# An attention and feed-forward block on one core: where the last splits of x are traced, and the last feature blocks of gate and up as a seven-product pair

## The chip, the cores and the metric

The kernel runs on one core of a Trainium2 chip. The metric is device time in microseconds, the median over runs. All arithmetic is float32; matmuls take their operands as float32 with rounded mantissa ("fp32r"), and a product that must be exact to float32 is made of three of them.

## The reference

One token block of 2048 rows (T) and 1024 columns (C) goes through an attention layer and a feed-forward layer, each with a layer norm ahead of it, a layer norm behind it and a residual:

```
x = x + layernorm(attention(layernorm(x)))   # one head, width 256
x = x + layernorm(ffn(layernorm(x)))
ffn(x) = (silu(x @ W_gate.T) * (x @ W_up.T)) @ W_down.T   # 2752 features
```

The feed-forward width of 2752 is 21 blocks of 128 features and a last piece of 64.

## The kernel before

**Three-fold products.** Every operand is split into a high part (a cast to fp32r, on ScalarE) and a low part (the source minus the high part, on VectorE). A block of a product is then three matmuls: high by high, high by low, low by high (`mmc`, L600 to L607, whose matmul is L605). The weight splits stand in `split` (L109 cast, L110 subtraction), those of x in `split_later` (L407 cast, L408 subtraction), whose two instructions are kept in their traced order against other work (`pin`).

**Stages.** First come q, k and v, then attention over 16 row tiles (`scores`, `softmax`, `turn`, `attend`, `turn_o`, `proj`), then, for each half s of the rows, gate and up (`gate_up`, then `gate_up_rest`) and the down product (`run_down`). The residual and layer norm of the last eight attention tiles run as background jobs inside the first half's gate and up. An instruction scheduler sets the final order on every engine from the traced order and its own estimates; each engine then works through its queue in order, and waits where an operand isn't ready.

**Seven products instead of eight.** A pair of feature blocks (p and p + 10) by two halves of rows and two halves of the inner dimension is a 2 x 2 by 2 x 2 block product. `gate_up` makes it with seven block products (Strassen's scheme in a form with few sums): the weight sums S1 to S4 are made on chip in `Pair.prep` (L529 to L532), the sums of x are called T1 to T4, the plain blocks A11 to A22 and B11 to B22. A `prod` is 4 inner blocks by 3 matmuls of 512 columns, 12 matmuls, into one PSUM bank. Gate and up of one pair are 14 `prod` calls over the four banks `ag`, `au`, `cg`, `cu`. Ten pairs cover 20 blocks. What is left over, block 20 of gate, block 20 of up, and the 64 last features of gate and of up side by side in one block (`wlast`), is done in `gate_up_rest` as three `Single` blocks with four `prod` calls each.

**Buffers of weights.** Split weights lie in six slots (four in `a2`, shown as `a`, and two in `wvo`, which held Wo during attention), raw weights in the four buffers `f4[4]`, `f2p[0]`, `f2p[1]`, `wr[0]` (shown as f, f2p, wr). A queue of loads and preparations (`Feeder`) is pumped whenever a slot comes free, at each `done()`.

**Buffers of x.** The split x of the current half lies in `xb` (B11, B21), `kx` (T1, T3), `qa` and `qb` (T2) and `a1` (T4, B22; shown as `a`, as `a2` is). `kx`, `qa`, `qb` and `a1` hold attention's keys, queries and values until it ends. For the first half, sums of x made during attention are stored to memory (`xs_d`), and ten pieces (`First` objects, in the list `order`) are loaded and split late: `order[0:4]` before the last `attend`, `order[4:6]` ahead of `turn_o(15)` and `proj(15)`, `order[6:10]` behind `proj(15)` and ahead of the first pair. They pass through four buffers, f4[2], f4[3], wr[1] and xe (`spare`). `order[4]` fills `qb`, `order[5]` the last of T1 and T3, `order[6:10]` T4 and B22.

**Names in the profile.** L276 and L277 are matmuls of `attend`, L279 and L280 gather its result, L285 is `turn_o`, L146 to L148 with wvo are `proj`, and L295 is its scaling and bias. L637 and L639 are the ScalarE copies that free banks `ag` and `au` after the first two products of a pair; L651 to L664 are the later copies, L618 is every sum on VectorE, L621 every silu, L347 the transposes of a background job.

Of the kernel before, what the change touches and what calls it, by code (L numbers as in the profile page):

```python
# [11 lines left out]
ALU = mybir.AluOpType  # L12
# [3 lines left out]
P = 128  # L16
# [10 lines left out]
FR = F - FB * P  # L27
NKB = T // P
EPS = 1e-5
NPAIR = 10  # L30
# [4 lines left out]
def block_kernel(ctx, tc, x, wqk, wv, bqk, bv, wo, bo, wgu, wlast, wd, out):  # L35
# [12 lines left out]
    nc = tc.nc  # L48
# [13 lines left out]
    bo_s = tl(cpool, [P, C], F32, "bo_s")  # L62
# [25 lines left out]
    hl_d = [[tl(dram, [FR, 512], F32, f"hl_d{s}_{k}") for k in range(2)] for s in range(2)]  # L88
# [5 lines left out]
    f4 = [tl(cpool, [P, C], F32, f"f4_{i}") for i in range(5)]  # L94
# [325 lines left out]
    class First:  # L420


        def __init__(self, dst, halves):
            self.dst, self.halves = dst, halves
# [69 lines left out]
    class Pair:  # L494


        def __init__(self, p, m):
            self.p, self.m = p, m
            self.s = {}
            one, two_, three, four = Slot(), Slot(), Slot(), Slot()  # L500
            self.slot = [one, two_, three, four]

            self.at = {"A11": (one, 0), "A12": (one, 4), "S2": (two_, 0), "S1": (two_, 4), "S3": (three, 0), "S4": (three, 4), "A22": (four, 0)}
# [3 lines left out]

        def load(self):
            self.r = [raws.get(), raws.get()]
            for r, fb in zip(self.r, (self.p, self.p + NPAIR)):  # L510
                nc.sync.dma_start(r.rearrange("p (c f) -> p c f", f=P), wgu[fb, self.m])
            self.loaded = True

        loaded = False
# [94 lines left out]
    def prod(o, w, a, b, first=True):  # L609

        slot, c0 = w.at[a]
        v = w4(slot.need())
        for cb in range(4):
            x = xq(b, cb)
            mmc(o, (v[:, c0 + cb, 0, :], v[:, c0 + cb, 1, :]), (x[:, 0, :], x[:, 1, :]), first and cb == 0, cb == 3, not first)

    def add(o, a, b, op=ALU.add):
        nc.vector.tensor_tensor(o, a, b, op)  # L618

    def silu(o, a):  # L620
        nc.scalar.activation(o, a, AF.Silu)  # L621

    def gate_up(s, p, wg, wu, bg, jobs):

        ag, au, cg, cu = bg
        g11, g12, g22, g21, u11, u12, u22 = tmp[0:7]
        job = list(jobs)

        def background():
            if job:  # L630
                job.pop(0)()

        def put(name, t):
            nc.sync.dma_start(hd[s][p][name], t)

        prod(ag, wg, "A11", "B11")
        nc.scalar.copy(g11, ag)  # L637
        prod(au, wu, "A11", "B11")
        nc.scalar.copy(u11, au)  # L639
        prod(cg, wg, "A12", "B21")  # L640
        wg.slot[0].done()
        add(g11, cg, g11)
        silu(g11, g11)
        prod(cu, wu, "A12", "B21")
        wu.slot[0].done()
        add(u11, cu, u11)
        add(g11, g11, u11, ALU.mult)
        put("A11", g11)
        background()
        prod(ag, wg, "S2", "T2", False)  # L650
        nc.scalar.copy(g12, ag)  # L651
        prod(au, wu, "S2", "T2", False)
        nc.scalar.copy(u12, au)
        prod(cg, wg, "S1", "T1")
        wg.slot[1].done()
        prod(cu, wu, "S1", "T1")
        wu.slot[1].done()
        background()
        prod(ag, wg, "S3", "T3", False)
        nc.scalar.copy(g22, ag)  # L660
        add(g22, cg, g22)
        silu(g22, g22)
        prod(au, wu, "S3", "T3", False)
        nc.scalar.copy(u22, au)  # L664
        add(u22, cu, u22)
        add(g22, g22, u22, ALU.mult)
        put("A22", g22)
        background()
        prod(ag, wg, "A22", "T4", False)
        wg.slot[3].done()  # L670
        silu(g21, ag)
        prod(au, wu, "A22", "T4", False)
        wu.slot[3].done()
        add(g21, au, g21, ALU.mult)
        put("A12", g21)
        prod(cg, wg, "S4", "B22", False)
        wg.slot[2].done()
        add(g12, cg, g12)
        silu(g12, g12)
        prod(cu, wu, "S4", "B22", False)  # L680
        wu.slot[2].done()
        add(u12, cu, u12)
        add(g12, g12, u12, ALU.mult)
        add(u22, g12, g22)
        add(u12, g11, g12, ALU.subtract)
        add(u11, u22, g11, ALU.subtract)
        add(g12, g21, u11, ALU.subtract)
        put("S1", u22)
        put("S3", u12)
        put("S2", u11)  # L690
        put("S4", g12)

    def gate_up_rest(s, wg, wu, wl, bg):
        ag, au, cg, cu = bg
        g11, g12, g22, g21, u11, u12, u22 = tmp[0:7]
        for w, a, c, u in ((wg, ag, cg, g12), (wu, au, cu, u12)):
            prod(a, w, "A11", "B11")
            nc.scalar.copy(u, a)
            prod(c, w, "A11", "T1")
        for w, a, c in ((wg, ag, cg), (wu, au, cu)):  # L700
            prod(a, w, "A12", "B21", False)
            prod(c, w, "A12", "B22", False)
            w.one.done()
        silu(g11, ag)
        add(g11, au, g11, ALU.mult)
        nc.sync.dma_start(hr_d[s][0], g11)
        add(g12, cg, g12)
        silu(g12, g12)
        add(u12, cu, u12)
        add(g12, g12, u12, ALU.mult)  # L710
        nc.sync.dma_start(hr_d[s][1], g12)
        prod(ag, wl, "A11", "B11")
        nc.scalar.copy(u11, ag)
        prod(cg, wl, "A11", "T1")
        prod(ag, wl, "A12", "B21", False)
        prod(cg, wl, "A12", "B22", False)
        wl.one.done()
        silu(g21[:FR, :], ag[:FR, :])
        add(g21[:FR, :], ag[FR : 2 * FR, :], g21[:FR, :], ALU.mult)
        nc.sync.dma_start(hl_d[s][0], g21[:FR, :])  # L720
        add(g22[:FR, :], cg[:FR, :], u11[:FR, :])
        silu(g22[:FR, :], g22[:FR, :])
        add(u22[:FR, :], cg[FR : 2 * FR, :], u11[FR : 2 * FR, :])
        add(g22[:FR, :], g22[:FR, :], u22[:FR, :], ALU.mult)
        nc.sync.dma_start(hl_d[s][1], g22[:FR, :])

    def load_down(p):
        for r, fb in zip(f4[0:2], (p, p + NPAIR)):
# [136 lines left out]
    X, Y = bank[0:4], bank[4:8]  # L865
    half = []
    for s in range(2):
        pairs = [(Pair(p, 0), Pair(p, 1)) for p in range(NPAIR)]
        rest = Single(wgu[2 * NPAIR, 0]), Single(wgu[2 * NPAIR, 1]), Single(wlast)
        dn = Down(s)  # L870
        half.append((pairs, rest, dn))
        for wg, wu in pairs:
            wg.queue_load()
            wu.queue_load()
            for i in range(4):
                wg.queue_prep(i)
                wu.queue_prep(i)
        for w in rest:
            w.queue_load()
            w.queue_prep(0)  # L880
        dn.queue()


# [1 line left out]
    for i in range(NT):  # L885
# [35 lines left out]
        if i == NT - 2:  # L921
# [4 lines left out]
            spare = f4[2], f4[3], wr[1], xe  # L926
            for f, r in zip(order, spare):
                f.load(r)
    for n in range(4, 6):
        order[n].load(spare[n % 4])  # L930
        order[n].use()
    turn_o(NT - 1)
    proj(NT - 1)
    for n in range(6, 10):
        order[n].load(spare[n % 4])
        order[n].use()
    spool.release()
    xipool = pool("xi")
    xi = [tl(xipool, [P, C], F32, f"xi{i}") for i in range(4)]
    y = f4[0:4] + xi  # L940
    tmp = [xi[i // 2][:, (i % 2) * 512 : (i % 2) * 512 + 512] for i in range(8)]
    raws2.free(wr[1])
    raws2.free(bo_s)
    for n in range(2, 4):
        slots.free(flat(a2[:, 2 * n : 2 * n + 2, :, :]))
    for n in range(2):
# [3 lines left out]
    def late(p):  # L950
        return EARLY + p if 0 <= p < NT - EARLY else None

    def ahead(p):

        if late(p - 1):
            xpose(late(p - 1), *f4[2:4], Y[0:2])
        if late(p):
            nc.sync.dma_start(f4[2], at_d[late(p)])
            nc.sync.dma_start(f4[3], x[late(p) * P : (late(p) + 1) * P, :])
        down_weights(p)  # L960

    def behind(p):
        if p + 1 < NPAIR:
            load_down(p + 1)
        if late(p):
            residual(late(p), *f4[2:4])

    load_down(0)
    for s in range(2):
        pairs, rest, dn = half[s]  # L970
        bg, other = (X, Y) if s == 0 else (Y, X)
        for p in range(NPAIR):
            jobs = [] if s else [lambda: ahead(p), lambda: behind(p)]
            gate_up(s, p, *pairs[p], bg, jobs)
        gate_up_rest(s, *rest, bg)

        def next_x(cb):
            r1, r2 = raws2.get(), raws2.get()
            build_x(2, cb, r1, r2)
            raws2.free(r1)  # L980
            raws2.free(r2)

        if s == 0:
            run_down(s, dn, other, bg, 2 * TB * [None], [lambda cb=cb: next_x(cb) for cb in range(4)])
        else:
            xpool.release()
            x1pool = pool("x1", side="right")
            x1 = [tl(x1pool, [P, C], F32, f"x1_{k}") for k in range(2 * TB)]
            run_down(s, dn, other, bg, x1, [lambda k=k: nc.sync.dma_start(x1[k], x1_d[2 * TB + k]) for k in range(2 * TB)])
# [39 lines left out]
```

## Time and profile before

| what | value |
|---|---|
| median of three runs | 1710.32 us (1709.04 to 1710.4) |
| the profiled execution | 1707.72 us |
| its span, first to last instruction | 1705.9 us |
| granted TensorE clock, mean | 0.991 |
| TensorE busy | 1678.0 us, 7788 matmuls |
| VectorE busy | 1090.9 us |
| ScalarE busy | 690.2 us |
| memory traffic | 271 MB, 159 GB/s |

The span is the profiled execution without what lies around it, 1.8 us here. PE stands for TensorE, DVE for VectorE, ACT for ScalarE, POOL for GpSimd, SP for SyncE, which issues nearly all transfers. A line of a wait list reads: engine, what it was about to do and its line, what it waited for, total us, times, longest us. A line of a timeline reads: start, duration, engine, line, operation, output and input, shapes, count, and in brackets the engine's idle time before it and what ended it.

### The profile page before, as it was taken

To read this page: it belongs to the slowest core of one execution; us is meant where nothing else is said; L and a number is where in the kernel's file an instruction comes from. 1 tells how busy PE (TensorE), PEld (TensorE's weight loads), DVE (VectorE), ACT (ScalarE), POOL (GpSimd) and SP (SyncE) were. 2 spreads that over 40 slices of the span, in tenths; PEclk is the share of its full clock that TensorE was granted. 3 is DMA by queue.
4 is the path that set the end of the run, shared out by engine and by line. 5 is a ranking of instruction groups with operands and counts; after the bars stand their busy time and mean duration, and the time that the engine had idled before them with its cause. 6 is when DMAs were issued, how large, how long until landed. Compare 5 with 4: busy or idle time off the path is not lost.

```text
span 1705.9 us, 21119 instructions
## 1 busy us (share of the span) xinstructions
PE 1678.0 (98%) x7788; PEld 1393.6 (82%) x7788; DVE 1090.9 (64%) x1666; ACT 690.2 (40%) x1031; POOL 93.4 (5%) x118
## 2 busy tenths in 40 slices
PE   8999999999899999999999999999999999999997
PEld 7888887888688888888888888888888888888886
DVE  8643667667877777776378457866555664445458
ACT  3222445544544444443356444433333333244343
POOL 1000000000011211110000000100000000000001
PEclk8999999999899999999999999999999999999999
DMA  6221123334765566665357656633332223475654
GB/s 213 81 81 37 38 75 124 100 123 172 241 216 197 202 214 216 218 214 190 132 196 243 205 192 194 215 107 115 134 109 93 93 93 124 147 279 189 196 190 159
DMA packets 131015, 271.01 MB, mean 159 GB/s; under 512 B 13280, under 2 KB 29792, under 8 KB 130912
## 3 DMA queue, kind: packets, MB, share of 16 engines
q1 hardware_dynamic: 128176, 262.72, 45.5%
q10 hardware_dynamic: 2736, 6.95, 1.2%
q8 instruction: 61, 1.00, 0.2%
q14 instruction: 42, 0.34, 0.1%
HBM read 185.73 MB, written 83.89 MB: 158 GB/s over the span
## 4 chain that ended last, share of the span: by engine, by line
PE 95%; DVE 2%; ACT 1%; issue 1%; DMA 1%; POOL 0%; POOLq 0%; DVEq 0%; ACTq 0%; SPq 0%
PE bank L605 72%; PE bank L147 4%; PE bank L146 4%; PE bank L148 4%; PE bank L276 3%; PE bank L277 2%; PE bank L206 2%; PE bank L268 1%; PE bank L207 1%; PE bank L347 1%; PE bank L139 1%; PE bank L774 0%; DVE small L116 0%; PE bank L775 0%; DMA f<-wv 0%
## 5 line engine op out<-in xcount | busy, mean ns | idle before, releaser
L605 PE MATMUL bank<-a 128*128 128x512 f32 x1176 | 272.7, 389 | 0.0
L605 PEld LDWEIGHTS bank<-a 128*128 128x128 f32 x1176 | 220.7, 188 | 45.9
L605 PE MATMUL bank<-xb,a 128*128 128x512 f32 x816 | 192.0, 389 | 0.0
L110 DVE TENSOR_TENSOR a<-f2p,a 128x1024 fp32r<-128x1024 f32 (+2 forms) x114 | 124.6, 1094 | 88.4 <-ACT a L109 76.4
L618 DVE TENSOR_TENSOR xi<-bank,xi 128x512 f32<-128x512 f32 (+1 forms) x168 | 112.8, 682 | 106.7 <-PE bank L605 64.7
L605 PEld LDWEIGHTS bank<-xb,a 128*128 128x128 f32 x816 | 153.1, 188 | 31.8
L605 PE MATMUL bank<-kx,a 128*128 128x512 f32 x648 | 152.9, 389 | 0.0
L109 ACT CAST a<-f2p 128x1024 fp32r<-128x1024 f32 (+2 forms) x114 | 108.2, 950 | 110.1 <-PE bank L605 98.7
L605 PE MATMUL bank<-a,a 128*128 128x512 f32 x648 | 152.6, 389 | 0.0
L110 DVE TENSOR_TENSOR a<-f,a 128x512 fp32r<-128x512 f32 (+3 forms) x93 | 91.4, 982 | 86.7 <-ACT a L109 81.8
L605 PEld LDWEIGHTS bank<-kx,a 128*128 128x128 f32 x648 | 121.6, 188 | 25.3
L605 PEld LDWEIGHTS bank<-a,a 128*128 128x128 f32 x648 | 121.6, 188 | 25.3
L605 PE MATMUL bank<-wvo 128*128 128x512 f32 x600 | 141.5, 389 | 0.0
L605 PEld LDWEIGHTS bank<-wvo 128*128 128x128 f32 x600 | 112.6, 188 | 23.4
L109 ACT CAST a<-f 128x512 fp32r<-128x512 f32 (+3 forms) x93 | 69.5, 747 | 122.3 <-PE bank L605 87.3
L276 PE MATMUL bank<-a,a 128*128 128x512 f32 x256 | 94.6, 403 | 2.8 <-ACT f L349 2.1
L110 DVE TENSOR_TENSOR wvo<-f2p,wvo 128x1024 fp32r<-128x1024 f32 (+2 forms) x48 | 54.7, 1140 | 64.8 <-ACT wvo L109 56.4
L605 PE MATMUL bank<-a,wvo 128*128 128x512 f32 x384 | 91.2, 389 | 1.2 <-ACT xi L664 1.2
L605 PE MATMUL bank<-kx,wvo 128*128 128x512 f32 x384 | 91.3, 389 | 0.0
L618 DVE TENSOR_TENSOR xi<-xi,xi 128x512 f32<-128x512 f32 x124 | 85.3, 688 | 4.3
L605 PEld LDWEIGHTS bank<-a,wvo 128*128 128x128 f32 x384 | 72.0, 188 | 16.5 <-ACT xi L664 1.6
L605 PEld LDWEIGHTS bank<-kx,wvo 128*128 128x128 f32 x384 | 72.1, 188 | 15.0
(234 smaller groups left out, 2748.9 us busy)
## 6 DMA issues: line engine op xcount, KB each, us to landing
f2p<-wgu SPq DMA_DIRECT2D x43, 512.0 KB, 4.9
hd_S<-xi SPq DMA_DIRECT2D x80, 256.0 KB, 4.4
f<-x SPq DMA_DIRECT2D x30, 512.0 KB, 3.8
hd_A<-xi SPq DMA_DIRECT2D x60, 256.0 KB, 2.0
f<-wgu SPq DMA_DIRECT2D x21, 512.0 KB, 4.7
wr<-wgu SPq DMA_DIRECT2D x20, 512.0 KB, 5.8
f<-wd SPq DMA_DIRECT2D x20, 512.0 KB, 4.5
td_T<-f SPq DMA_DIRECT2D x40, 256.0 KB, 4.8
```

The costliest lines, as they stand in the source:

```text
L109: nc.scalar.copy(hi, src)
L110: (lo_engine or nc.vector).tensor_tensor(lo, src, f32(hi), ALU.subtract)
L139: nc.tensor.transpose(b[:, j * P : (j + 1) * P], t[:, cb * P : (cb + 1) * P], ident)
L146: nc.tensor.matmul(o, w[0], m[0], start=first, stop=False)
L147: nc.tensor.matmul(o, w[0], m[1], start=False, stop=False)
L148: nc.tensor.matmul(o, w[1], m[0], start=False, stop=last)
L206: nc.tensor.matmul(b, xg[:, c, 0, cols], wv_s[:, c, :, :].rearrange("p a f -> p (a f)"), start=(c == 0), stop=False)
L207: nc.tensor.matmul(b[:, D:], xg[:, c, 1, cols], wv_s[:, c, 0, :], start=False, stop=(c == 7))
L276: nc.tensor.matmul(b, p[:, k, 0, :], vt[:, k, :, :].rearrange("p h d -> p (h d)"), start=(k == 0), stop=False)
L277: nc.tensor.matmul(b[:, D:], p[:, k, 1, :], vt[:, k, 0, :], start=False, stop=(k == NKB - 1))
L605: one = nc.tensor.matmul(o, w[i], m[j], start=first and n == 0, stop=last and n == 2, skip_group_check=chained)
L618: nc.vector.tensor_tensor(o, a, b, op)
```

## The change

It has two parts.

1. **The pair of last blocks.** `Pair` takes its two sources as arguments instead of computing them from p and m. The rest of a half becomes one `Pair` of gate's block 20 and `wlast`, with seven products, and one `Single` for up's block 20, with four: 11 `prod` calls instead of 12. `gate_up_rest` is rewritten for it. The pair's preparations are queued as part 0, then up's block, then parts 1 to 3.
2. **The last splits of x.** `order[4:6]` are split in a new background job `first`, called inside the first pair after the copies L637 and L639; `order[6:10]` are split at the start of the job `ahead`, after the pair's first store. `bo_s`, which `proj` reads, takes the place of xe as the fourth buffer of the loads of `order[4:10]`, and the loads of `order[8:10]` are traced inside `first`.

```diff
-        def __init__(self, p, m):
-            self.p, self.m = p, m
+        def __init__(self, *src):
+            self.src = src
...
+        background()                      # in gate_up, after the copy of u11
         prod(cg, wg, "A12", "B21")
...
-    def gate_up_rest(s, wg, wu, wl, bg):
...
+    def gate_up_rest(s, wp, wu, bg):
+        ap, au, cp, cu = bg
+        prod(ap, wp, "A11", "B11")
+        nc.scalar.copy(g11, ap)
+        prod(au, wu, "A11", "B11")
+        nc.scalar.copy(u12, au)
+        prod(cp, wp, "A12", "B21")
+        wp.slot[0].done()
...
+        prod(cu, wu, "A11", "T1")
+        prod(ap, wp, "S2", "T2", False)
+        nc.scalar.copy(g12, ap)
+        prod(au, wu, "A12", "B21", False)
...
+        prod(cp, wp, "S1", "T1")
+        wp.slot[1].done()
+        prod(cu, wu, "A12", "B22", False)
+        wu.one.done()
...
+        prod(ap, wp, "S3", "T3", False)
+        nc.scalar.copy(g22, ap)
...
+        prod(ap, wp, "A22", "T4", False)
+        wp.slot[3].done()
...
+        prod(cp, wp, "S4", "B22", False)
+        wp.slot[2].done()
...
-        rest = Single(wgu[2 * NPAIR, 0]), Single(wgu[2 * NPAIR, 1]), Single(wlast)
+        rest = Pair(wgu[2 * NPAIR, 0], wlast), Single(wgu[2 * NPAIR, 1])
...
-    for n in range(4, 6):
-        order[n].load(spare[n % 4])
-        order[n].use()
     turn_o(NT - 1)
     proj(NT - 1)
-    for n in range(6, 10):
-        order[n].load(spare[n % 4])
-        order[n].use()
+    last = f4[2], f4[3], wr[1], bo_s
+    for n in range(4, 8):
+        order[n].load(last[n % 4])
...
+    def first(p):
+        if p == 0:
+            for n in range(4, 6):
+                order[n].use()
+                order[n + 4].load(last[n % 4])
+
     def ahead(p):
+        if p == 0:
+            for n in range(6, 10):
+                order[n].use()
+            raws2.free(wr[1])
+            raws2.free(bo_s)
...
-            jobs = [] if s else [lambda: ahead(p), lambda: behind(p)]
+            jobs = [] if s else [lambda: first(p), lambda: ahead(p), lambda: behind(p)]
```

More of the change, by code (lines that the diff above doesn't have):

```diff
@@ L509, in load @@
             self.r = [raws.get(), raws.get()]
-            for r, fb in zip(self.r, (self.p, self.p + NPAIR)):
-                nc.sync.dma_start(r.rearrange("p (c f) -> p c f", f=P), wgu[fb, self.m])
+            for r, w in zip(self.r, self.src):
+                nc.sync.dma_start(r.rearrange("p (c f) -> p c f", f=P), w)
             self.loaded = True
@@ L691, in gate_up @@
         put("S4", g12)
-    def gate_up_rest(s, wg, wu, wl, bg):
-        ag, au, cg, cu = bg
+    def gate_up_rest(s, wp, wu, bg):
+        ap, au, cp, cu = bg
         g11, g12, g22, g21, u11, u12, u22 = tmp[0:7]
[L696 to L704, printed above, removed]
+        prod(ap, wp, "A11", "B11")
[4 more added lines that the diff above has]
+        wp.slot[0].done()
+        add(g11, cp, g11)
+        silu(g11, g11)
+        prod(cu, wu, "A11", "T1")
+        prod(ap, wp, "S2", "T2", False)
+        nc.scalar.copy(g12, ap)
+        prod(au, wu, "A12", "B21", False)
@@ L705, in gate_up_rest @@
         add(g11, au, g11, ALU.mult)
         nc.sync.dma_start(hr_d[s][0], g11)
-        add(g12, cg, g12)
+        prod(cp, wp, "S1", "T1")
+        wp.slot[1].done()
+        prod(cu, wu, "A12", "B22", False)
+        wu.one.done()
+        add(u12, cu, u12)
+        prod(ap, wp, "S3", "T3", False)
+        nc.scalar.copy(g22, ap)
+        add(u22[:FR, :], cp[FR : 2 * FR, :], g22[FR : 2 * FR, :])
+        add(g22[:FR, :], cp[:FR, :], g22[:FR, :])
+        silu(g22[:FR, :], g22[:FR, :])
+        add(g22[:FR, :], g22[:FR, :], u22[:FR, :], ALU.mult)
@@ L708, in gate_up_rest @@
+        nc.sync.dma_start(hl_d[s][1], g22[:FR, :])
+        prod(ap, wp, "A22", "T4", False)
+        wp.slot[3].done()
+        silu(g21[:FR, :], ap[:FR, :])
+        add(g21[:FR, :], ap[FR : 2 * FR, :], g21[:FR, :], ALU.mult)
+        nc.sync.dma_start(hl_d[s][0], g21[:FR, :])
+        prod(cp, wp, "S4", "B22", False)
+        wp.slot[2].done()
+        add(g12, cp, g12)
         silu(g12, g12)
-        add(u12, cu, u12)
         add(g12, g12, u12, ALU.mult)
         nc.sync.dma_start(hr_d[s][1], g12)
-        prod(ag, wl, "A11", "B11")
@@ L713, in gate_up_rest @@
[L713 to L724, printed above, removed]
@@ L725, in gate_up_rest @@
-        nc.sync.dma_start(hl_d[s][1], g22[:FR, :])
     def load_down(p):
@@ L867, in block_kernel @@
     for s in range(2):
-        pairs = [(Pair(p, 0), Pair(p, 1)) for p in range(NPAIR)]
-        rest = Single(wgu[2 * NPAIR, 0]), Single(wgu[2 * NPAIR, 1]), Single(wlast)
+        pairs = [tuple(Pair(wgu[p, m], wgu[p + NPAIR, m]) for m in range(2)) for p in range(NPAIR)]
+        rest = Pair(wgu[2 * NPAIR, 0], wlast), Single(wgu[2 * NPAIR, 1])
         dn = Down(s)
@@ L879, in block_kernel @@
             w.queue_load()
-            w.queue_prep(0)
+        wp, wu = rest
+        wp.queue_prep(0)
+        wu.queue_prep(0)
+        for i in range(1, 4):
+            wp.queue_prep(i)
         dn.queue()
@@ L941, in block_kernel @@
     tmp = [xi[i // 2][:, (i % 2) * 512 : (i % 2) * 512 + 512] for i in range(8)]
-    raws2.free(wr[1])
-    raws2.free(bo_s)
     for n in range(2, 4):
```

## The prediction

> **What bounds the kernel now.** I read the page's busy table first, then TensorE's waits, then the stretches around its longest wait.
>
> ```profile
> PE 1678.0 (98%) x7788; PEld 1393.6 (82%) x7788; DVE 1090.9 (64%) x1666; ACT 690.2 (40%) x1031; POOL 93.4 (5%) x118
> ```
>
> TensorE is busy for 98% of 1705.9 us, so a matmul less is time less wherever no wait takes its place. What a matmul costs comes from the chain of work: its piece "688.30 38.10 PE bank L605 x168" gives 38.10 / 168 = 0.2268 us from one to the next (a row's mean of 389 ns holds the overlap and isn't the price).
>
> Idle time is 28 us. TensorE's list of waits says where a change of order could find some of it:
>
> ```profile
> PE bank L605 <- ACT xi L637: 4.3, 1, 4.3
> ...
> PE bank L146 <- DVE oTs L110: 2.3, 2, 1.8
> ...
> PE bank L605 <- ACT xi L664: 1.2, 1, 1.2
> ...
> PE bank L146 <- ACT oTs L109: 0.9, 1, 0.9
> ```
>
> The waits of 4.3, 1.8 and 0.9 us all lie between the end of attention and the first pair of gate and up. Busy time by stretch (TensorE first, granted clock as a share, then the DMA share):
>
> ```profile
> 436.00:440.00 4.00, 3.73 (x20) 2.73 (x18) 1.97 (x4) 2.12 (x4) 0.00 (x0) 1.00 0.46 164
> 440.00:444.00 4.00, 1.31 (x4) 0.80 (x4) 4.00 (x7) 3.34 (x5) 0.00 (x0) 0.82 0.59 203
> 444.00:448.00 4.00, 4.00 (x10) 2.63 (x8) 2.27 (x5) 1.86 (x3) 0.00 (x0) 0.50 0.91 321
> 448.00:452.00 4.00, 0.11 (x1) 0.00 (x0) 4.00 (x6) 2.74 (x4) 0.00 (x0) 0.50 0.89 299
> 452.00:456.00 4.00, 3.56 (x8) 2.81 (x9) 4.00 (x5) 2.16 (x3) 0.00 (x0) 0.50 0.63 222
> ```
>
> The clock is halved from about 443.5 to 456 us: ten matmuls in the third row where 17 would fit. The timeline shows why TensorE stood still, in ScalarE's order:
>
> ```profile
> 438.67 1.05 ACT L407 CAST qb<-f 128x1024 fp32r<-128x1024 f32 x1
> 439.62 1.04 ACT L407 CAST kx<-f 128x1024 fp32r<-128x1024 f32 x1
> ...
> 440.56 0.37 ACT L109 CAST oTs<-bank 128x256 fp32r<-128x256 f32 x1
> ...
> 443.00 0.42 DVE L110 TENSOR_TENSOR oTs<-bank,oTs 128x256 fp32r<-128x256 f32 x1
> ...
> 450.86 1.04 ACT L407 CAST a<-f 128x1024 fp32r<-128x1024 f32 x1 [1.26 <-DMA f<-xT_d]
> ...
> 451.81 0.58 ACT L637 COPY xi<-bank 128x512 f32<-128x512 f32 x1
> 452.44 2.93 PE L605 MATMUL bank<-qa,a 128*128 128x512 f32 x6 [4.33 <-ACT xi L637]
> ```
>
> The copy at L637 frees the bank of the first product. That product was long done, but the copy stands in ScalarE's queue behind the splits of x (L407), whose last waits for its transfer.
>
> Reckoned as one stretch: turn_o(15) starts at 439.62 and the second pair's transposes at 492.56, 52.9 us. The work in it is turn_o (0.4), 12 matmuls of proj(15) and 168 of the pairs, 180 x 0.2268 + 0.4 = 41.2 us. So **11.7 us are lost**: 7.0 of idling (0.93 + 1.76 + 4.33), 2.0 of half clock in the products (40.12 instead of 38.10 for the 168), some 2.2 in proj(15) (10 matmuls about 0.43 apart), the rest drains.
>
> [...]
>
> **Part one, the rest of each half.** Before, three single blocks each take four products: 12 x 12 = 144 matmuls. After, the pair takes seven and up's block four: 132. Two halves: 24 fewer, 24 x 0.2268 = **5.4 us**, all on TensorE, with no idle time in that stretch (837 to 925 us) now.
>
> What it adds per half is off TensorE. VectorE: the pair's four sums (4 x 0.61, the spacing of such adds in the timeline) and its splits, 3.5 rather than two 1024-column pieces (1.5 x 1.14 = 1.7), about 4 us against 30 us of products. ScalarE: 1.5 x 0.95 = 1.4 us. Transfers: the same three 512 KB weight loads, the same four stores. Slots: the ring has six; the pair takes four, up's block one, where the singles took three. By the order of the calls to done(), each down step still gets its slot at least five products (13.6 us) ahead, against a load of 4.9 us, a cast of 1.05 and a subtraction of 1.22, 7.2 us. So I cost this at nothing. The next x of the second half is built from xb, kx, qa and a1, which are now read some products longer; down runs 240 us beside it.
>
> **Part two, the last six splits.** They are traced inside the first pair instead of ahead of it: two after the copies of the first products, four after the first store. In the compiled order one cast (from wr[1]) has moved ahead, into a gap of 2.1 us where ScalarE waited for attend; the others follow L637 and L639. I walk the queues with the trace's spacing (1.14 us for a 1024-column subtraction, 0.61 for a 512-column one, 0.95 and 0.5 for the casts):
>
> - oTs: its cast follows turn_o directly, 440.15 to 440.5; VectorE then does one sum, and the low half at 441.2. proj(15) starts at 440.6 (0.5 idle) and waits 0.2 more: ends 443.7, at full clock.
> - ScalarE: the cast into wvo must wait for wo_s, read by proj(15): 443.2 to 444.2; a weight cast to 444.85; L637 to 445.45, L639 to 445.9, qb to 446.9, kx to 447.9. **First product of the new group at 445.6** instead of 452.44: 1.9 idle.
> - VectorE: up's S2 low half at 446.7, bank reads at 447.3 and 447.9, qb low half 451.2, kx 452.4. TensorE wants these at about 447.4, 448.9, 451.2, 453.4 and 455.7 in the new order, which puts other products ahead of the late halves: none is late.
> - SP: bo_s takes the place of xe and can only be refilled after proj(15) reads it (issue 445.7 to 446.4, landing by 451.5). The last two loads (four DMAs, 256 KB each) now queue behind the load of f4[1] at L739, which waits for the at_d store to land (5.6 us before): issue 452.5 to 454, landing at 457 to 459. ScalarE then casts at 458.4 and 459.4, VectorE ends at 461.5 and 463.3. T4 wants them at about 463.6 and 466.6. **Some 2 us of slack, the thinnest part.**
>
> Loss that remains: 0.5 + 0.2 + 1.9 = 2.6 us. I add 1.0 for VectorE: my list of its queue from 440 us to the first reads of the second pair is 41.5 us (12 x 1.14, 38 x 0.61, small ones) beside 46 us on TensorE, so late(0)'s sums come just when the second pair wants its banks. I add 0.8 for the clock[...]. Together 4.4, so 11.7 - 4.4 = **7.3 us** gained. Bounds: 2.0 lost (9.7 gained) to 9.0 lost (2.7 gained).
>
> **Sum.** 5.4 + 7.3 = 12.7. The profiled execution took 1707.7 (span 1705.9), so 1695.0; the median shown, 1710.3, is 2.6 above it: **1697.6 us**. The case's own range is 1694 to 1701.
>
> **Rivals.**
> - *The wait moves into the first pair.* If the last x loads land 3 to 6 us later than I have them (DMA share is 0.9 in 444 to 452) or VectorE falls behind, ScalarE stands at the cast with the copies L661 and L665 behind it, and TensorE waits before T4. For it: loads took up to 5.0 us, weight loads 5.6. Against: the 2 us of slack, a transfer-poor stretch after 452. Gain 5.4 + 2: 1703, between 1701 and 1705.
> - *Part two is eaten whole and some of part one.* Half clock through the first pair and a wait in each rest: a gain under 3.4 us, 1707 to 1713.
> - *Slower: down starves for slots.* If the pair's four slots are held until its end, two remain for down's steps, 2 x 2.72 = 5.4 us of products against 7.2 us to fill one: 1.8 us lost a step. It decides from eight steps in all, over 14 us; twelve steps would lose 22: 1719. Against: the order of done() frees slots after the third and seventh product.
> - *The change doesn't do what it says.* If all six splits still ran ahead of L637, 5.4 us alone: 1705. The compiled order speaks against it; I count it with the first rival.
>
> **How the numbers follow.** First case 0.70, a gain above its range 0.02, first rival 0.18, second 0.05, slower 0.05. Runs here differ by about 0.1%, so 0.2%, 3.4 us, is what can be told from no change. Faster 0.90, same 0.05, slower 0.05. The range takes the first case and the better part of the first rival: 1694 to 1704.
>
> **What would show it.** Right: 24 fewer L605 matmuls; the wait on L637 at 1 to 3 us and those before L146 under 1; TensorE without a gap through both rests; the 168 matmuls of the pairs in about 39 us. Wrong: a wait of over 3 us on L661, L665 or a cast L407 inside the first pair; half clock past 450 us; TensorE waiting for a split at L109 in the first down steps.

## The result, and the profile after

| | before | after |
|---|---|---|
| median, first comparison (6 runs each) | 1709.68 us | 1699.58 us |
| ratio to before, with its interval | | 0.9944 [0.9931, 0.9957] |
| profiled execution | 1707.72 us | 1700.9 us |
| its span | 1705.9 us | 1699.1 us |

The change makes the kernel 9.6 us faster (0.0056 x 1709.68). Two further comparisons below gave 0.9945 and 0.9942. The forecast was 1697.6 us, between 1694 and 1704. The two profiled executions are only 6.8 us apart: that of before lies at the fast end of its runs, that of after at the slow end. What the trace locates is therefore those 6.8 us, not the 9.6.

The busy table after:

```profile
PE 1669.2 (98%) x7764; PEld 1385.5 (82%) x7764; DVE 1100.3 (65%) x1682; ACT 694.8 (41%) x1039; POOL 91.3 (5%) x118
```

7788 - 7764 = 24 matmuls are gone, and VectorE has 9.4 us more work. A piece of the chain of waits still gives the price of a matmul, 38.10 / 168 = 0.2268 us, and two of its long pieces show part one. The chain before:

```profile
532.41 38.10 PE bank L605 x168
...
923.12 111.52 PE bank L605 x492
...
1109.32 435.49 PE bank L605 x1920
```

And after:

```profile
530.29 38.10 PE bank L605 x168
...
918.27 111.52 PE bank L605 x492
...
1104.86 432.82 PE bank L605 x1908
```

From such a x168 piece to the first x492 piece lie gate and up from the third pair on, the first rest and the beginning of down: 390.71 us before (532.41 to 923.12), 387.98 after, 2.73 less. The longest piece, with the second rest in it, is 432.82 instead of 435.49 us with 12 matmuls fewer, 2.67 less. Together 5.4 us.

TensorE's list of waits after (what it was about to do, what it waited for, total us, times, longest):

```profile
PE bank L605 <- ACT xi L637: 3.1, 2, 1.6
PE bank L605 <- ACT xi L661: 2.6, 1, 2.6
...
PE bank L285 <- DVE f L280: 1.3, 1, 1.3
PE bank L605 <- ACT xi L665: 1.2, 1, 1.2
PE bank L605 <- ACT xi L639: 1.0, 1, 1.0
...
PE bank L146 <- DVE oTs L110: 0.5, 1, 0.5
...
PE bank L146 <- ACT oTs L109: 0.5, 1, 0.5
```

The wait of 4.3 us is gone and the waits before L146 in this place are down from 2.7 to 0.5 us (the 0.5 on L110 is an earlier tile's), but four new ones stand around it: 1.3 before turn_o (L285, 0.3 before), 2.6 on L661, a second wait on L637, 1.0 on L639. (The 1.2 on L665 is in the second half, and was on L664 before.) From the end of attention through the second pair this is 1.3 + 0.5 + 3.1 + 2.6 + 1.0 = 8.5 us of idling, against 0.3 + 0.9 + 1.8 + 4.3 = 7.3 before.

What went away in this profile is the half clock. Busy time in steps of 4 us (after the step's length TensorE, its weight loads, VectorE, ScalarE, GpSimd; then the granted clock as a share, the DMA share and GB/s):

```profile
436.00:440.00 4.00, 2.99 (x16) 2.21 (x14) 0.92 (x3) 1.84 (x3) 0.00 (x0) 1.00 0.05 20
440.00:444.00 4.00, 3.23 (x13) 2.25 (x14) 3.96 (x8) 1.16 (x3) 0.00 (x0) 1.00 0.53 173
444.00:448.00 4.00, 2.54 (x12) 1.77 (x11) 4.00 (x7) 4.00 (x6) 0.00 (x0) 1.00 0.59 195
448.00:452.00 4.00, 4.00 (x20) 3.30 (x19) 3.39 (x5) 3.12 (x4) 0.00 (x0) 1.00 0.91 316
452.00:456.00 4.00, 4.00 (x19) 3.34 (x18) 3.41 (x4) 1.64 (x2) 0.00 (x0) 1.00 0.96 337
```

The third row held ten matmuls at half clock and the fourth one; now 12 and 20 at full clock. The cure isn't complete: in the two further profiles of the changed kernel below, the clock was 0.65 in 444 to 448 us and 0.57 in 464 to 468. For all runs below I use one measure: **the stretch**, from where TensorE begins to wait for turn_o(15) to the first product of the third pair. It is 93.1 us before and 91.3 after. So of the 6.8 us between the profiles 5.4 are part one, and only 1.8 part two; the other stages are 0.4 us longer in sum.

The timeline shows where the new waits come from. First ScalarE at the end of attention:

```profile
437.63 1.05 ACT L407 CAST a<-wr 128x1024 fp32r<-128x1024 f32 x1 [2.21 <-PE bank L277]
438.59 0.61 ACT L109 CAST a<-wr 128x512 fp32r<-128x512 f32 x1
439.11 0.36 ACT L279 COPY f<-bank 128x256 f32<-128x256 f32 x1
...
445.30 0.58 ACT L637 COPY xi<-bank 128x512 f32<-128x512 f32 x1
445.78 0.59 ACT L639 COPY xi<-bank 128x512 f32<-128x512 f32 x1
```

The one split of x that was moved ahead did not run inside the 2.2 us in which ScalarE waited. It ran behind them, because its own destination, an `a` buffer, is read by the last products of attend (L277), and the copy L279 then had to wait for it. Then ScalarE, VectorE and TensorE inside the first pair:

```profile
462.29 1.05 ACT L407 CAST a<-f 128x1024 fp32r<-128x1024 f32 x1 [3.56 <-DMA f<-xT_d]
...
463.59 1.04 ACT L407 CAST a<-f 128x1024 fp32r<-128x1024 f32 x1 [0.26 <-DMA f<-xT_d]
464.54 0.58 ACT L661 COPY xi<-bank 128x512 f32<-128x512 f32 x1
...
465.17 1.20 PE L605 MATMUL bank<-a,a 128*128 128x512 f32 x4 [2.62 <-ACT xi L661]
```

ScalarE stands 3.56 us at a cast whose transfer has not landed, with L661, which frees a bank, two places behind it. And in the second pair:

```profile
483.51 2.96 POOL L304 TENSOR_TENSOR f<-f,f 128x1024 f32<-128x1024 f32 x1 [1.37 <-DMA f<-wd]
...
484.40 3.16 DVE L110 TENSOR_TENSOR wvo<-f2p,wvo 128x1024 fp32r<-128x1024 f32 x1 [0.19 <-ACT wvo L109]
487.48 0.68 DVE L618 TENSOR_TENSOR xi<-xi,xi 128x512 f32<-128x512 f32 x1
...
488.19 0.59 ACT L637 COPY xi<-bank 128x512 f32<-128x512 f32 x1 [3.83 <-DVE xi L618]
488.83 1.66 PE L605 MATMUL bank<-qa,a 128*128 128x512 f32 x6 [1.60 <-ACT xi L637]
```

A subtraction that takes 1.22 us elsewhere takes 3.16 beside an addition on GpSimd; the sums behind it are late, so L637 is late, and TensorE waits 1.60 us.

### The profile page after: what moved, and what is told of

It reads as the page before. It is cut to its first block, busy times and chain, and to the rows that moved or that the text cites. A ratio compares the mean times of both kernels' runs of the same rounds, so it can differ in the third digit from the quotient of the medians.

```text
span 1699.1 us, 21099 instructions
## 1 busy us (share of the span) xinstructions
PE 1669.2 (98%) x7764; PEld 1385.5 (82%) x7764; DVE 1100.3 (65%) x1682; ACT 694.8 (41%) x1039; POOL 91.3 (5%) x118
## 4 chain that ended last, share of the span: by engine, by line
PE 92%; DVE 4%; DMA 2%; ACT 1%; issue 1%; POOL 0%; SPq 0%; POOLq 0%; DVEq 0%; ACTq 0%
PE bank L605 69%; PE bank L146 4%; PE bank L147 4%; PE bank L148 4%; PE bank L276 3%; PE bank L277 2%; PE bank L206 2%; PE bank L268 1%; PE bank L207 1%; PE bank L347 1%; PE bank L139 1%; DVE a L110 1%; DVE small L116 0%; DMA f<-xT_d 0%; DVE wvo L110 0%
## 5 line engine op out<-in xcount | busy, mean ns | idle before, releaser
L605 PE MATMUL bank<-xb,a 128*128 128x512 f32 x912 | 212.3, 389 | 0.1
L605 PEld LDWEIGHTS bank<-xb,a 128*128 128x128 f32 x912 | 171.1, 188 | 36.0 <-ACT xi L621 0.6
L110 DVE TENSOR_TENSOR a<-f2p,a 128x1024 fp32r<-128x1024 f32 (+2 forms) x133 | 134.6, 1012 | 58.0 <-ACT a L109 54.0
L109 ACT CAST a<-f2p 128x1024 fp32r<-128x1024 f32 (+2 forms) x133 | 117.5, 884 | 131.7 <-PE bank L605 107.2
L110 DVE TENSOR_TENSOR a<-f,a 128x1024 fp32r<-128x1024 f32 (+2 forms) x91 | 89.9, 988 | 106.5 <-ACT a L109 99.8
L605 PE MATMUL bank<-a,a 128*128 128x512 f32 x588 | 140.2, 390 | 3.8 <-ACT xi L661 2.6
L605 PEld LDWEIGHTS bank<-a,a 128*128 128x128 f32 x588 | 110.2, 188 | 27.5 <-ACT xi L661 3.0
L109 ACT CAST a<-f 128x1024 fp32r<-128x1024 f32 (+2 forms) x91 | 69.5, 764 | 141.6 <-PE bank L605 110.3
L605 PE MATMUL bank<-a,wvo 128*128 128x512 f32 x444 | 106.3, 389 | 0.0
L605 PEld LDWEIGHTS bank<-a,wvo 128*128 128x128 f32 x444 | 83.3, 188 | 17.3
L276 PE MATMUL bank<-a,a 128*128 128x512 f32 x256 | 94.6, 403 | 2.8 <-ACT f L349 2.0
L110 DVE TENSOR_TENSOR wvo<-f,wvo 128x1024 fp32r<-128x1024 f32 (+1 forms) x52 | 60.8, 1169 | 54.9 <-ACT wvo L109 53.8
L618 DVE TENSOR_TENSOR xi<-xi,xi 128x512 f32<-128x512 f32 (+1 forms) x124 | 85.3, 688 | 5.6 <-ACT xi L621 1.5
```

Of the source, the lines that this page charges most:

```text
L109: nc.scalar.copy(hi, src)
L110: (lo_engine or nc.vector).tensor_tensor(lo, src, f32(hi), ALU.subtract)
L276: nc.tensor.matmul(b, p[:, k, 0, :], vt[:, k, :, :].rearrange("p h d -> p (h d)"), start=(k == 0), stop=False)
L605: one = nc.tensor.matmul(o, w[i], m[j], start=first and n == 0, stop=last and n == 2, skip_group_check=chained)
```

## The experiments

My theory: part one gives the whole of its 5.4 us; part two removes the half clock, but its saved waits come back as the four just seen. The rivals: part one brings the half-clock cure by itself; the four waits are not what costs; the half clock is not due to TensorE's standing still. Every time is a median, and every ratio is to runs of the kernel before on the same chip.

| run | time, us | ratio to before | stretch, us |
|---|---|---|---|
| part one alone | 1702.49 | 0.9963 [0.995, 0.9976] | 93.6 |
| part two alone | 1706.55 | 0.9989 [0.9981, 0.9997] | 89.5 |
| changed kernel again | 1698.19 | 0.9945 [0.9933, 0.9958] | 91.8 |
| changed kernel, third comparison | 1697.85 | 0.9942 [0.9929, 0.9954] | 92.4 |
| down's first load later | 1699.89 | 0.995 [0.9938, 0.9962] | 90.3 |
| a buffer of its own for x | 1695.98 | 0.9934 [0.9921, 0.9946] | 87.7 |
| sums one pair later | 1699.74 | 0.9948 [0.9935, 0.9962] | 89.8 |
| cast kept behind | 1697.89 | 0.9943 [0.9931, 0.9956] | 89.7 |
| combined | 1694.87 | 0.9923 [0.991, 0.9937] | 85.3 |
| combined, again | 1694.05 | 0.992 [0.9906, 0.9933] | 85.2 |
| before, filled with 8 + 30 transposes | 1704.9 | 0.998 [0.9973, 0.9986] | 92.0 |
| before, filled with 8 + 48 transposes | 1706.23 | 0.9985 [0.9979, 0.9992] | 90.9 |

Where the sums come one pair later (both kernels with that edit), 0.87 us are added to the stretch for the set of transposes that left it. Line numbers of the experiments differ from the changed kernel's by up to two.

The stretch varies by itself: with the same code of part two it is 89.5 us in the profile of part two alone and 91.3, 91.8 and 92.4 in the changed kernel's three. A stretch inside these bounds says nothing about an edit by its length; the single waits, and values well outside, do.

**Each part alone.** The kernel before with the new pair of last blocks, and the changed kernel with the old rest:

```diff
+        rest = Pair(wgu[2 * NPAIR, 0], wlast), Single(wgu[2 * NPAIR, 1])    # part one alone
...
+        rest = Single(wgu[2 * NPAIR, 0]), Single(wgu[2 * NPAIR, 1]), Single(wlast)    # part two alone
```

> Part one alone: the kernel before with the rest of each half as pair and single block, the last splits of x still ahead of the first pair. Theory A (part one is worth its 24 matmuls, part two only some 2 to 5 us): 5.4 us faster than before, a ratio of 0.9968, with the 4.3 us wait on L637 and the half clock after attention still there and no wait in the rests. Theory B (part two is worth the 7.3 us that were reckoned, and the rests eat half of part one): 2 to 3 us faster, ratio about 0.9985, with a wait or a gap on TensorE in the rests or in down.

> Part two alone: the last six splits of x traced inside the first pair, the rest of each half still as three single blocks of four products. Theory A: 2 to 5 us faster (ratio 0.997 to 0.999), TensorE at full clock after attention, but waits of 2.6 us on L661 before T4 and of 1 to 2 us at the start of the second pair. Theory B: 7 us faster, ratio 0.9959.

> The changed kernel once more, on the same chip as the others of this group, so that they can be compared: about 10 us faster than before (ratio 0.994). If the parts add up, its gain is the sum of the gains of the two parts. Under both theories the wait on L661 before T4 is 2 to 3 us and the copy L637 of the second pair comes 1 to 2 us late.

Part one alone gains 6.3 us (4.1 to 8.5 by its interval), part two alone 1.9 (0.5 to 3.2), both together 9.4: they add up within their intervals. In its profile part two alone takes 3.6 us from the stretch and loses 1.9 again behind it: 1.4 between the halves, where TensorE waits 1.2 us on silu's line (L621) as the second half begins, and 0.5 at the end. Part one alone has such a wait too (1.1 us); the kernel before and the changed kernel don't. Part one alone keeps the wait on L637 and the half clock. From its waits:

```profile
PE bank L605 <- ACT xi L637: 4.9, 1, 4.9
```

and from its steps of 4 us:

```profile
452.00:456.00 4.00, 3.69 (x9) 2.92 (x10) 4.00 (x4) 2.03 (x3) 0.00 (x0) 0.50 0.66 235
```

So the cure of the clock belongs to part two, and the rival that part one brings it falls.

**The late transfers.** Down's first loads (`load_down(0)`), traced ahead of the first pair, are issued behind the last load of x:

```diff
...
-                order[n + 4].load(last[n % 4])
+                dma = order[n + 4].load(last[n % 4])
+            with tc.issue_after(dma.ins):
+                load_down(0)
...
-    load_down(0)
```

> The changed kernel with the first two loads of down's weights (f4[0] and f4[1]) issued behind the last loads of x instead of ahead of them, so that nothing on SP's queue waits for the at_d store ahead of the x loads. Theory A (the wait on L661 comes from SP's queue: the x loads are issued 2.5 us late and behind 512 KB more): the wait on L661 falls from 2.6 to under 0.5 us, about 2 us faster than the changed kernel. Rival (the transfers are slow because all queues are full then, whatever the order): the wait stays at 2 us or more and the time is that of the changed kernel. Second rival (the wait moves on): L661 is freed, but the second pair's start waits as much longer, since VectorE is the one that is behind: no gain.

The last loads of x were issued 3 us earlier, landed in 5.4 to 5.9 us instead of 7.3 to 7.8, and the wait on L661 is gone. The time didn't improve, since in the compiled order the cast now stood ahead of an earlier copy:

```profile
457.19 1.04 ACT L407 CAST a<-f 128x1024 fp32r<-128x1024 f32 x1 [5.16 <-DMA f<-xT_d]
458.14 0.58 ACT L653 COPY xi<-bank 128x512 f32<-128x512 f32 x1
...
458.77 4.61 PE L606 MATMUL bank<-kx,wvo 128*128 128x512 f32 x12 [2.27 <-ACT xi L653]
```

ScalarE waits longer than before, 5.16 us, and TensorE 2.27, after which the clock fell (0.68 in 460 to 464 us). The place of a cast in ScalarE's queue matters as much as the landing. In the next kernel xe is kept beside bo_s as a fifth buffer, so that one of the two last loads (`order[8]`) is issued as soon as `order[3]` has been split, well before the first pair:

```diff
...
+    order[8].load(xe)
...
-    xi = [tl(xipool, [P, C], F32, f"xi{i}") for i in range(4)]
+    xi = [tl(xipool, [P, C], F32, f"xi{i}") for i in range(3)] + [xe]
...
-                order[n + 4].load(last[n % 4])
+            order[9].load(f4[2])
```

> The changed kernel with xe kept as a fifth buffer: order[8] is loaded there as soon as order[3] has been split, instead of into f4[2] after order[4], so only order[9] is loaded late. SP's queue is as it was. Theory A (L661 waits for late transfers): the wait on L661 falls from 1.8 to 2.6 us to under 1, up to 2 us faster than the changed kernel. Rival (the last of the two loads decides and queues as before): the wait stays at 1.5 us or more.

One late load is left, the wait on L661 is 0.7 instead of 2.6 us, and the stretch is 3.6 us shorter than in the first profile of the changed kernel. This is the largest effect of one edit, and the only one clearly outside the spread. By the ratios it is 1 to 2 us of time, which their intervals don't tell from nothing.

**The late sums.** late(p), which makes VectorE's and GpSimd's residual work, is moved one pair later:

```diff
-        return EARLY + p if 0 <= p < NT - EARLY else None
+        return EARLY + p - 1 if 0 <= p - 1 < NT - EARLY else None
```

> The changed kernel with the background residuals begun one pair later (the eight late tiles in pairs 1 to 8 instead of 0 to 7), so that VectorE and GpSimd have no layer norm to do in the first pair. Theory A (the late start of the second pair, 1.6 us on L637 and 1.0 on L639, comes from that work: VectorE behind by then, a 1.2 us subtraction stretched to 3.2 beside GpSimd's addition, transposes waiting for the layer norm): both waits fall under 0.5 us, some 2 us faster than the changed kernel (1696.5); the wait on L661 stays at 1.5 to 2.6. Rival (VectorE is behind because of the splits of x alone): the wait on L637 stays over 1 us and the time within 0.7 us of the changed kernel's.

The second pair's subtraction is back to its price, with no GpSimd work beside it, and the second pair's wait on L637 is gone:

```profile
480.91 1.21 DVE L110 TENSOR_TENSOR wvo<-f2p,wvo 128x1024 fp32r<-128x1024 f32 x1
...
484.57 0.59 ACT L637 COPY xi<-bank 128x512 f32<-128x512 f32 x1 [1.95 <-DVE xi L618]
...
493.49 0.59 ACT L639 COPY xi<-bank 128x512 f32<-128x512 f32 x1 [6.94 <-DMA hd_S<-xi]
```

The mechanism holds, but the 2 us that were expected did not come: the time is that of the changed kernel. The copy L639 now waited 6.94 us for a store of its buffer (1.1 us for TensorE), and the wait on L661 was 3.6 in this profile.

**The cast that moved ahead.** The splits of order[6:10] are held behind the cast of order[5], so that none can run before turn_o:

```diff
...
-            for n in range(6, 10):
-                order[n].use()
+            with tc.issue_after(order[5].cast.ins):
+                for n in range(6, 10):
+                    order[n].use()
```

> The changed kernel with the casts of T4 and B22 issued behind the cast of order[5] on ScalarE, so that the cast from wr[1] no longer stands ahead of L279. Theory A (that cast waited for the end of attend and put L279, and with it turn_o, off by 0.7 to 1 us): the wait of 0.6 to 1.4 us ahead of turn_o (L285) falls to 0.3, first product of the group about 0.5 to 1 us earlier, time at most 1 us better. Rival (the cast lies on ScalarE's path in any place; put behind, it delays L652 by as much): no gain, and a new wait on L652 of about 1 us.

L279 starts at 437.95 instead of 439.11, and the wait before turn_o is 0.3 us again. The stretch, 89.7 us, lies within the spread, and the ratio moved by nothing that its interval can tell.

**All four together**, with the four splits placed by hand (two behind the cast of order[5], two behind the store of the first pair):

```diff
+            with tc.issue_after(order[5].cast.ins):
+                for n in range(6, 8):
+                    order[n].use()
...
+        if p == 0:                            # in behind(p)
+            for n in range(8, 10):
+                order[n].use()
```

> All of it together: xe as a fifth buffer, down's first weights loaded behind the last x load, the casts of order[6:8] behind order[5]'s, those of order[8:10] traced in the later job (behind L652 and L654), the residuals one pair later. Theory A (about 8.9 us of waits between attention's end and the third pair, of which these remove those before turn_o, on L661, and at the second pair's start): 3 to 6 us faster than the changed kernel, 1693 to 1696, with only the wait of about 1.5 us on the first L637 and 1 us in proj(15) left. Rival (each wait gives way to the next, because VectorE has 41 us of work there): under 2 us faster.

> The combined version once more (x's fourth buffer of its own, loaded early; the four splits behind the cast of order[5]; sums of late one pair later; the first load of down issued behind the last x load), beside the changed kernel in the same call. Theory (what part two left lies in the four waits, and they can be had together): again about 1695, 3 to 4 us faster than the changed kernel, with the stretch from turn_o to the third pair at 85 to 86 us against its 91 to 92. Rival (the two values came from different calls and a good part of the difference was the chip's): under 2 us between them.

> The changed kernel unaltered, as the measure for the combined version: 1698 to 1700, ratio 0.9945 to before; the waits before T4 (L661), on L637 in both pairs and on L285 as in its first profile, 7 to 9 us in sum with the others between turn_o and the third pair.

On one chip beside the changed kernel the combined version takes 1694.05 against 1697.85 us: 3.8 us faster, and 14 faster than before. From its waits (L639 is here what was L637, and L667, at the start of the second half, what was L665):

```profile
PE bank L607 <- ACT xi L639: 1.5, 1, 1.5
...
PE bank L607 <- ACT xe L667: 1.2, 1, 1.2
```

The waits on L661 and on L637 in the second pair are gone, and the one before turn_o is back at 0.3 us; the stretch, 85.2 us, is 7.2 shorter than that of the changed kernel beside it. The two profiles are 4.7 us apart. Of the 7.2 us, 1.6 were lost ahead of the stretch, in a part whose length also differs by 1.8 between two profiles of the changed kernel (it ends at 438.99 and at 440.76 us), 0.2 in gate and up and 0.8 between the halves. In part these 0.8 are the wait on silu's line as the second half begins (0.4 us here, 0.9 in the first profile of the combined version). Each part alone has it too, so it doesn't take the shifted sums to bring it; its cause stays open.

**The half clock.** The kernel before, with transposes of the identity that nobody reads, so that TensorE is busy while it has no product to make:

```diff
+    def fill(n):
+        for _ in range(n):
+            pin(nc.tensor.transpose(bank[6][:, 0:P], ident, ident))
...
     turn_o(NT - 1)
+    fill(8)
     proj(NT - 1)
+    fill(30)            # 48 in the second
```

> The kernel before, with TensorE given something to do while it has no products: 8 transposes of the identity into a bank that nobody reads, behind turn_o(15), and 30 behind proj(15). Nothing else changes; ScalarE still reaches L637 behind the same splits. Theory (the half clock of 443.5 to 456 us comes from TensorE standing still, and part two's gain is that clock and not the wait): the granted clock stays near 1.00 from 444 to 460 us, proj(15) runs at about 0.23 us a matmul and the 168 products of the pairs take about 38.2 us instead of 40.1, while the wait on L637 stays at 4 us or a little more in sum with the filling; 2 to 4 us faster than before, ratio about 0.998. Rival one (the clock is halved for another reason, such as the load of the other engines or of the DMAs): clock 0.50 from 444 to 456 as before, and 0 to 2 us slower for the filling. Rival two (clock restored but the wait grows by as much, since ScalarE sets the end of it and its own work waits for transfers): clock 1.00, the 168 products faster by 2 us, the whole within 1 us of before.

> As the kernel with the filling of 8 and 30 transposes, with 48 behind proj(15) instead of 30. With 30 the filling ended at 449.5 us, TensorE stood still for another 2.1 us before the first product that waits for L637, and the clock was 0.58 in 452 to 456, so that the 168 products took 40.0 us. Theory (half the clock follows TensorE's standing still, here in two places): 18 transposes more at 0.115 us cover those 2.1 us; the wait on L637 is under 0.5 us, the clock 1.00 in all stretches from 444 to 460, the 168 products take 38.1 to 38.3 us, and the stretch from turn_o to the third pair is 1.5 to 2 us shorter than with 30, 2.6 to 3.1 shorter than before: 1.5 to 2 us faster than with 30 in the profile. Rival (the clock falls there because of what the other engines do): clock 0.5 to 0.6 in 452 to 456 again and 40 us for the products; as with 30, or slower by the filling.

With 30, TensorE still stood 2.13 us ahead of L637's release, and the expectation of a full clock to 460 us missed: it fell to 0.58 in 452 to 456, and the products took 39.99 us. With 48 that gap is covered:

```profile
440.00:444.00 4.00, 2.06 (x13) 1.37 (x12) 4.00 (x6) 4.00 (x6) 0.00 (x0) 1.00 0.56 187
444.00:448.00 4.00, 3.85 (x23) 3.35 (x24) 3.97 (x8) 1.45 (x3) 0.00 (x0) 1.00 0.87 321
448.00:452.00 4.00, 3.99 (x37) 3.75 (x35) 4.00 (x4) 3.48 (x6) 0.00 (x0) 1.00 0.99 391
452.00:456.00 4.00, 3.87 (x17) 3.22 (x18) 4.00 (x6) 1.37 (x4) 0.00 (x0) 1.00 0.82 273
```

The clock is full in all four rows. From 444 to 456 us the DMA share is 0.87, 0.99 and 0.82, before 0.91, 0.89 and 0.63, and VectorE is busy for 11.97 of the 12 us, before for 10.27; so in this stretch standing still is the cause, not the other engines' load. The first products begin at 452.13 us, the second pair's transposes at 490.34: 38.2 us instead of the 40.0 with 30. The first product that needs L637 starts 11.8 us after turn_o instead of 12.8. **Useless transposes alone shorten the stretch by 2.2 us and the time by 2.6 (1.4 to 3.6)**, in time as much as part two alone (1.9), which takes 3.6 from the stretch. Against 8 + 30 the expected 1.5 to 2 us did not come: the stretch is 1.1 us shorter, and the ratios, 0.9985 and 0.998, don't differ by their intervals. 8 + 30 gained 3.4 us by its median and 2.1 between the profiles: 1.1 of these are in the stretch, and a wait of 1.2 us on L664 at the start of the second half was missing in that profile.

## Why the prediction was right in sum, and wrong in part two

**Part one: exact.** 24 matmuls at 0.2268 us were forecast at 5.4; the trace has 2.73 + 2.67 = 5.4, and there is no new wait in either rest. Costing the added sums, casts and slots at nothing held: VectorE's 9.4 us more lie beside products. The slower rival (down starves for slots) did not come: no wait on L109 in the first down steps.

**Part two: right mechanism, over-sized.** Forecast 7.3 us with bounds of 2.7 to 9.7. Measured in time 1.9 alone, and 3.1 as what part one leaves of 9.4; in the stretch 1.8, 1.3 and 0.7 in the changed kernel's three profiles, and 3.6 alone. Most of these lie under the low bound, and all are at most half of the forecast. The first rival's 2 us for part two are nearer. Term by term:

- *The clock*: I left 0.8 us of the 4.2 at half clock, an estimate of mine. In the first profile it vanished wholly. In the second it came back (0.65 in 444 to 448, after waits of 1.4 before turn_o and 0.5 behind it; proj(15)'s matmuls lay 0.43 us apart instead of 0.23 up to 446.8 us), in the third too (0.57 in 464 to 468, after a wait of 3.0 on L661). Right, with luck in which profile; what the luck hangs on isn't shown. It took no long gap: the half clock before began at 442.6 us, not at 443.5, inside the second gap (1.76 us) and behind a first of 0.93.
- *The first product behind L637*: forecast at 445.6, seen at 445.93. The queue walk of ScalarE held here, although turn_o came later than it had it.
- *The cast from wr[1]* "moved ahead, into a gap of 2.1 us": **this step failed.** I took the gap as usable and did not ask what the cast's destination waits for. Its buffer came free at the gap's end; turn_o came 1.0 us later than it had to (1.3 of waiting instead of 0.3; 1.4 and 0.7 in the other two profiles). Keeping the cast behind removed it.
- *The last two loads*: issue forecast at 452.5 to 454, seen at 454.2 to 455.7. Landing forecast at 457 to 459, seen at about 462 to 463.5, because I gave them some 5 us where they took 7.3 to 7.8, at a DMA share of 0.95 to 0.96 up to 460 us, where I had counted on a transfer-poor stretch. **This term was mis-sized**, and my test of it was wrong as well: I compared the splits with T4's need at 463.6, but TensorE waited for a bank, which L661 frees behind those casts. That is the first rival's mechanism, with 2.6 us instead of "over 3"; a fifth buffer took 1.9 of it away.
- *VectorE, 1.0 us*: seen 1.6 in the second pair and 1.0 on L639. I counted VectorE's work at its undisturbed prices, and it left no slack for a subtraction of 3.16 us. Moving the sums removed the 1.6.

The forecast gain of 7.3 us was there to be had, but it took the four edits together: the combined version's stretch is 93.1 - 85.3 = 7.8 us shorter than before's.

**The sum.** The forecast for a profiled execution was 1695.0, and it took 1700.9: 5.9 us off, of which part two's shortfall in the stretch (7.3 - 1.8 = 5.5) is nearly all. The 2.6 us that I added to reach a median were nearly right for the kernel before (2.0 by its six runs), but the profile of after lay above its median and not below. So the forecast median came within 2.0 us partly by luck: two errors had opposite signs.

## What to carry to other kernels

When a block of work is moved out of a queue's way, look at two things for each instruction that moves: what frees its destination, and which bank-freeing copies stand behind it while it waits for its transfer. Price a transfer by what else is in flight where it will run: here the same loads took 7.3 to 7.8 us behind down's load and 5.4 to 5.9 ahead of it. Before hunting the waits of TensorE, fill them with idle work once: what that alone gives, here 2.2 of the 3.6 us that part two alone takes from the stretch, was lost in the clock and not in the waits.

## What was not expected of the hardware

**The length of a gap alone didn't decide over the clock.** One gap of 3.6 us left it at 1.00 (the sums one pair later), as did one of 2.6 (after); 2.3 (down's load later) brought 0.68, 3.0 (changed kernel, third) 0.57, and before, 0.93 and 1.76 close together 0.50, from 442.6 to 456.2 us. Nor does TensorE's busy time in the row of 4 us from 460 to 464 us tell two of them apart: with 1.93 us in it the clock stayed at 1.00 (the sums one pair later), with 1.87 it fell in the next row to 0.57 (changed kernel, third). What else decides isn't shown by these profiles.

**Beside a GpSimd addition a VectorE subtraction took 3.16 us instead of 1.22.** GpSimd's addition, 2.96 us long, ended at 486.47, the subtraction at 487.56, 1.09 us later. Before, beside the addition at 476.69, a smaller subtraction took 2.48 us instead of 0.69, where nobody waited for it. A VectorE sum that read one operand from a bank, inside a GpSimd addition at 515.21 us before, took its usual 0.68 us. What sets the two cases apart isn't shown.
